# Fifteen products in place of eighteen for six of fc1's tiles, and convolution taps clipped to the image, in a two-layer fp32 kernel

## The chip, the cores and the metric

The kernel runs on one core of a Trainium2 chip, all in fp32. The metric is the device time of one execution in microseconds; the median of eight runs before the change is 3315.88 us (3313.56 to 3318.15). TensorE (PE in the profile) multiplies, VectorE is DVE, ScalarE is ACT, GpSimd is POOL, and SyncE (SP) issues most transfers.

## The reference

Eight images of 384 channels and 32x32 pixels (1024 tokens) go through two layers.

- Layer 0 is a transformer block: layernorm, qkv, attention with 8 heads of 48, projection and residual, layernorm, then an MLP, `fc1` from 384 to 1536 with exact GELU, `fc2` back to 384, and a residual.
- Layer 1 is a ConvNeXt block: a depthwise 7x7 convolution with 3 pixels of zero padding, layernorm over channels, `w1` to 1536, GELU, a global response normalisation (GRN) over the image, `w2` back to 384, and a residual.

The steps that the change touches are these:

```python
h = gelu(einsum('bnc,oc->bno', xn2, w_fc1) + b_fc1)
...
y = conv_general_dilated(x, dw_w, padding=((3, 3), (3, 3)), feature_group_count=DIM) + dw_b
```

## The kernel before

**Layout.** Channels lie on the 128 partitions, tokens along the free axis. 384 channels are three tiles (`CT`), 1536 hidden channels twelve (`HT`), and the 1024 tokens are worked in two halves of 512. The constant `NH` is 512.

**Order of the images.** The loop over images (in `main`, from L1420) is skewed: while image b goes through layer 0, layer 1 of image b-1 follows it. A turn of the loop is: q and k of image b, its attention, its MLP, then `grn_up` (w1) of image b-1, the values of image b+1, and `grn_down` (w2) of image b-1. The depthwise convolution of image b is started behind `grn_up` and runs on DVE beside the values, `grn_down`, and the whole attention of image b+1, up to the MLP of image b+1. The last image (b = 7) has another MLP, `mlp_by_halves`, and its own convolution in two parts of 13 and 19 rows at the end.

**The planner.** Each engine executes its instructions in the order in which the program emits them. `Flow` (L112) decides that order. Every matmul adds its cost to a running clock (`U`, 0.857 us for 512 columns), and chains of other work (generators that yield how long to wait) are resumed when the clock passes their due time. So a yield does not delay an engine; it decides behind which matmul, and between which other DVE instructions, a step stands. `finish` runs the rest of a chain at once. A paced chain counts its waits from when it was due.

**The convolution.** `convolution` (L959) emits 126 taps for a full image, 42 for each channel tile, as one DVE instruction each: acc = window x weight + acc, with a window of the zero-padded copy `pad` (38x38) and 1024 elements. Seven more taps for each channel tile are made by ACT and added by accumulating transfers that POOL issues (`help_convolution`, L985), channel tile after channel tile from the last to the first. While the helper is at a channel tile, and for 8 us after, `convolution` leaves it alone. The helper pauses where `quiet` is set (in w2 and at the averages of the attention). The layernorm of the convolved image (`conv_norm`) waits for the convolution, the helper and the layernorm in front of the MLP.

**fc1 and fc2.** `mlp` (L796) makes the first token half of all 12 hidden tiles, then the second half. A tile and half is three matmuls of 512 columns into one PSUM bank (four such banks rotate) and one GELU from the bank to `hid` (`gelu_half`, L778). Four tiles into the first half come the projection of the second half of the attention and the second half of the layernorm. Two `difference` calls prepare sums for fc2, each a negated copy on ACT and an accumulating transfer from POOL. fc2 and w2 are already made by a scheme of 15 block products in place of 18 (`by_thirds`, `FORMS` at L74): sums of weight blocks, made once, times sums of data blocks, with DVE combining the products.

**Weights.** A ring of nine tiles is loaded in the order of a plan by SP; `used` gives a tile back and issues the next load. An fc1 chunk holds two hidden tiles. During image 0 the chain `prepare` (L1261) makes the weight sums for qk, fc2, w1 and w2 on DVE and stores them to DRAM through POOL; `forms` (L1296) makes the fifteen forms for fc2 and for w2, and w2's come last. `main` finishes `prepare` behind the MLP of image 0 and then starts the first convolution.

Of the kernel before, what the change touches and what calls it, by code (L numbers as in the profile page):

```python
# [46 lines left out]
F32 = mybir.dt.float32  # L47
# [17 lines left out]
CM = 2  # L65
NC = HT // CM
U = 0.857
HELPED = 7
SCALE = HD ** -0.5
EPS0, EPS1, GRN_EPS = 1e-5, 1e-6, 1e-6  # L70
# [81 lines left out]
def block_kernel(  # L152
# [25 lines left out]
    flow = Flow()  # L178
    quiet = []
    s_fc2 = dram.tile([P, len(FORMS), 4 * P], F32, tag="s_fc2", bufs=1, name="s_fc2")  # L180
    s_w2 = dram.tile([P, len(FORMS), 4 * P], F32, tag="s_w2", bufs=1, name="s_w2")
    s_qk = dram.tile([P, CT, 4 * P], F32, tag="s_qk", bufs=1, name="s_qk")
    s_w1 = dram.tile([P, HT // 2, 4, P], F32, tag="s_w1", bufs=1, name="s_w1")

    def half(h):
        return slice(h * NH, (h + 1) * NH)
# [103 lines left out]
    def chunk(w, c):  # L290
        return w[:, c * 6 * P : (c + 1) * 6 * P]
# [1 line left out]

    RAW = ("A11", "A12", "A21", "A22", "A31", "A32")

    def plan_fc1(tag):
        return [((f"fc1_{tag}", c), chunk(wfc1, c)) for c in range(NC)]

    def plan_fc2(tag):
        return [((f"fc2_{tag}", a), chunk(wfc2, c)) for c, a in enumerate(RAW)]  # L300
# [482 lines left out]
    def difference(dst, more, less):  # L783

        nc.scalar.mul(dst, less, -1.0)
        nc.gpsimd.dma_start(out=dst, in_=more, accum_op=ALU.add)
# [5 lines left out]
    def add_first(xt, r, n, bank):  # L792
        dst = xt[:, r, half(n)]
        nc.vector.scalar_tensor_tensor(dst, bank, col("bfc2", r), dst, ALU.add, ALU.add)  # L794

    def mlp(b, xt, xn, weights, tag, ln, rest, before_fc2=None, behind_ln=None):  # L796

        hid = one.tile([P, HT * N], F32, tag="big", name=f"hid_{b}").rearrange("p (m n) -> p m n", m=HT)
        e = [three.tile([P, 2, NH], F32, tag="p", name=f"fc2_e_{b}_{i}") for i in range(2)]
        wa = f"fc1_{tag}"  # L800
        flow.finish(ln)
        for m in range(HT):
            gelu_half(hid, m, 0, xn, weights, wa, f"fc1_{b}")
            if m == 3 and rest:
                rest()
                slow = 1.2 if b == 1 else 1.0
                ln = flow.spawn(layernorm(xt, xn, 1, eps0, "g2", f"ln2_{b}", True, slow=slow))
                behind_ln(ln)
        flow.finish(ln)
        for m in range(HT):  # L810
            gelu_half(hid, m, 1, xn, weights, wa, f"fc1_{b}")
            if m % CM == CM - 1:
                weights.used(wa, m // CM)
            if m in (3, 5):
                two_tiles = hid[:, m - 3 : m - 1, :]
                difference(e[(m - 3) // 2], two_tiles[:, :, half(0)], two_tiles[:, :, half(1)])
        if before_fc2:
            before_fc2()
        bias = lambda r: col("bfc2", r)
        by_thirds(xt, hid, e, True, weights, f"fc2_{tag}", bias, lambda r, n: pad_half(xt, r, n), f"fc2_{b}")  # L820
# [132 lines left out]
    def keep(b, xt):  # L953
# [2 lines left out]
        nc.sync.dma_start(out=kept.rearrange("(c p) n -> p c n", p=P), in_=xt)  # L956
        return kept

    def convolution(acc, us, first=(), y0=0, y1=H, ready=tuple(range(CT)), taken=None):  # L959

        done = [0] * CT
        ct, n = None, 0
        taps = KS * KS - (HELPED if taken is not None else 0)
        while min(done) < taps:
            left = [c for c in ready if done[c] < taps and not (taken and taken.get(c, 0) > flow.now)]
            if not left:
                yield 1.0
                continue  # L970
            ct = min([c for c in left if c != ct] or left, key=lambda c: done[c])
            i = done[ct]
            dy, dx = divmod(i, KS)
            window = pad[:, ct, dy + y0 : dy + y1, dx : dx + W]
            dst = image(acc[:, ct, :])[:, y0:y1, :]
            tap = col("dww", ct * KS * KS + i)
            if i == 0:
                nc.vector.tensor_scalar(dst, window, tap, col("dwb", ct), ALU.mult, ALU.add)  # L978
            else:
                nc.vector.scalar_tensor_tensor(dst, window, tap, dst, ALU.mult, ALU.add)  # L980
            done[ct] += 1
            n += 1
            yield next((early for m, early in first if n <= m), us)

    def help_convolution(acc, us, taken):  # L985

        yield 8.0
        for ct in reversed(range(CT)):
            taken[ct] = float("inf")
            for i in range(KS * KS - HELPED, KS * KS):  # L990
                dy, dx = divmod(i, KS)
                for h in range(2):
                    if quiet:
                        while quiet:
                            yield 1.0
                        yield 3.0
                    t = three.tile([P, NH], F32, tag="res", bufs=4, name=f"tap_{ct}_{i}_{h}")
                    y0 = dy + h * H // 2
                    window = pad[:, ct, y0 : y0 + H // 2, dx : dx + W]
                    tap = col("dww", ct * KS * KS + i)  # L1000
                    nc.scalar.mul(t.rearrange("p (h w) -> p h w", w=W), window, tap)  # L1001
                    nc.gpsimd.dma_start(out=acc[:, ct, half(h)], in_=t, accum_op=ALU.add)  # L1002
                    yield us
            taken[ct] = flow.now + 8.0
        yield 8.0
        taken.clear()
# [254 lines left out]
    def prepare(weights, aside):  # L1261
# [17 lines left out]
        def load_blocks(w, name, *which):  # L1279
            t = one.tile([P, CT, N], F32, tag="acc", name=name).rearrange("p c n -> p (c n)")  # L1280
            parts = []
            for j, (m, k) in enumerate(which):
                parts.append(t[:, j * 4 * P : (j + 1) * 4 * P])
                nc.gpsimd.dma_start(out=parts[j], in_=block_of(w, m, k))
            return parts

        def spare(name):
            return three.tile([P, NH], F32, tag="res", bufs=4, name=name)
# [5 lines left out]
            nc.vector.tensor_tensor(dst, x, y, ALU.add)  # L1294

        def forms(name, w, store):  # L1296
            def keep_form(i, t):
                nc.gpsimd.dma_start(out=store[:, i, :], in_=t)

            a11, a12, a31, a33, a13, a23 = load_blocks(w, f"{name}_a", (1, 1), (1, 2), (3, 1), (3, 3), (1, 3), (2, 3))  # L1300
            x, y, z = (spare(f"{name}_{k}") for k in "xyz")
            yield 16.0
            add(a23, a23, a33)
            add(a11, a11, a12)
            keep_form(6, a11)
            sub(a31, a31, a11)
            keep_form(0, a31)
            yield 2.0
            add(x, a11, a13)
            sub(x, x, a23)  # L1310
            keep_form(8, x)
            nc.vector.scalar_tensor_tensor(y, a11, -1.0, a33, ALU.mult, ALU.subtract)
            keep_form(5, y)
            yield 2.0
            sub(z, a23, a12)
            keep_form(11, z)
            sub(a13, a13, a12)
            sub(a13, a13, a33)
            keep_form(13, a13)
            yield 2.0  # L1320
            nc.vector.tensor_scalar(a12, a12, -1.0, None, ALU.mult)
            keep_form(12, a12)
            nc.vector.tensor_scalar(a23, a23, -1.0, None, ALU.mult)
            keep_form(14, a23)
            a21, a22, a31, a32, a33, a12 = load_blocks(w, f"{name}_b", (2, 1), (2, 2), (3, 1), (3, 2), (3, 3), (1, 2))
            x, y = spare(f"{name}_v"), spare(f"{name}_w")
            nc.gpsimd.dma_start(out=x, in_=block_of(w, 2, 3))
            yield 25.0
            add(x, x, a33)
            sub(y, a22, x)  # L1330
            keep_form(7, y)
            add(a12, a12, a21)
            add(a12, a12, a31)
            keep_form(9, a12)
            yield 2.0
            add(a22, a21, a22)
            sub(a33, a33, a22)
            keep_form(2, a33)
            add(a22, a22, a31)
            keep_form(4, a22)  # L1340
            add(a32, a32, a22)
            keep_form(1, a32)
# [61 lines left out]
            nc.gpsimd.dma_start(out=s_w1[:, :, int(key[1]) - 1, :], in_=t[:, j])  # L1404
        yield from shift_through_w2()
        yield from forms("w2", w2, s_w2)

    def first_values(xn):

# [10 lines left out]
    def main():  # L1420
# [17 lines left out]
        plan = plan_fc1(0) + plan_fc2_fast(0) + plan_qk(1)  # L1438
        for b in range(1, B):
            if b < B - 1:  # L1440
                plan += plan_fc1(b) + plan_fc2_fast(b)
            else:
                for h in range(2):
                    plan += plan_fc1(f"{b}_{h}") + plan_fc2(f"{b}_{h}")
            plan += plan_w1(b - 1, b < B - 1)
            if b == B - 1:
                plan += plan_w1(f"{b}_0", False)
            plan += plan_w2(b - 1, b < B - 1)
            if b < B - 1:
                plan += plan_qk(b + 1)  # L1450
# [74 lines left out]
        for b in range(B):  # L1525
# [22 lines left out]
            flow.finish(state["norm3"])  # L1548
            if b < B - 1:
                y, gx = grn_up(b - 1, acc, weights, b - 1)  # L1550
                start_conv(b, 1.65 if b == B - 2 else 1.7, (26, 2.2), (27, 9.0), (35, 4.4))
                scale = flow.spawn(grn_scale(b - 1, gx, weights, b - 1, y))
                next_values(b + 1)
                flow.finish(scale)
# [166 lines left out]
```

## Time and profile before

| | |
|---|---|
| median of 8 runs | 3315.88 us (3313.56 to 3318.15) |
| the profiled execution | 3316.41 us, its span 3314.6 us |
| TensorE busy | 3278.0 us, 99% |
| DVE busy | 2512.0 us, 76% |
| ACT busy | 1604.2 us, 48% |
| POOL busy | 484.1 us, 15% |
| a turn of the loop, images 3 to 6 | 400.6 us |
| fc1's second half in the fourth image | 1336.4 to 1367.3 us |

Spans of PE's matmuls are modelled at the end: a matmul of 512 columns reads as 0.59 us while the next starts 0.43 us after it. An fp32 matmul stands as two passes, so two records. In a group's line, `out<-in` names the tiles, then come the shapes, the number of instructions, busy time, the mean of one in ns, and the idle time in front of them with what ended most of it. In a timeline a line is: start, duration, engine, line, operation, tiles, how many were merged, and in brackets the idle time in front of the first.

### The profile page before, as it was taken

What the parts mean: (1) busy time and instruction counts of PE and PEld (TensorE: products, weight loads), DVE (VectorE), ACT (ScalarE), POOL (GpSimd) and SP (SyncE); (2) the same over time, 40 slices, a digit from 0 to 9 for tenths busy, and PEclk for the clock granted to TensorE, in tenths of its full rate; (3) what the DMA queues carried; (4) which work ended last, traced back from release to release, by engine and by line L of the source; (5) the groups of instructions that cost most, each with busy time, mean ns of one, the idle gap of its engine ahead of it and who ended that gap; (6) DMA issues with size and microseconds to landing.
All of it is one profiled execution on the core that took longest, in us unless ns stands there. A gap on an engine that the chain in (4) does not pass through costs nothing. (4 is left out here: it accounts for less than half of the span.)

```text
span 3314.6 us, 38765 instructions
## 1 busy us (share of the span) xinstructions
PE 3278.0 (99%) x14296; PEld 1418.0 (43%) x14296; DVE 2512.0 (76%) x3186; ACT 1604.2 (48%) x2194; POOL 484.1 (15%) x569
## 2 busy tenths in 40 slices
PE   8999999999999999999999999999999999999998
PEld 4344444443344433444344443444434443444455
DVE  4445897888967978679786798868886888879950
ACT  2542663447534375353652737526474355623541
POOL 2121210112110121101211022111220112100000
PEclk9999999999999999999999999999999999999999
DMA  5336732647244563537436374273742647333231
GB/s 197 112 107 148 150 67 71 159 114 149 56 104 134 137 127 56 132 106 171 85 58 147 104 182 74 59 176 87 176 77 50 181 104 158 66 74 89 67 97 43
DMA packets 199109, 368.73 MB, mean 111 GB/s; under 512 B 40768, under 2 KB 46784, under 8 KB 198528
## 3 DMA queue, kind: packets, MB, share of 16 engines
q0 software_dynamic: 80896, 158.63, 26.4%
q1 hardware_dynamic: 117728, 206.83, 20.4%
q8 instruction: 115, 1.88, 0.2%
q10 hardware_dynamic: 288, 0.71, 0.1%
q14 instruction: 82, 0.67, 0.1%
HBM read 187.03 MB, written 34.60 MB: 67 GB/s over the span
## 5 line engine op out<-in xcount | busy, mean ns | idle before, releaser
L980 DVE SCALAR_TENSOR_TENSOR acc<-pad,vec,acc 128x1024 f32<-128x1024 f32 x861 | 1069.8, 1277 | 22.2 <-DMA acc<-tap 17.5
L673 ACT ACTIVATE p<-s 128x1024 f32<-128x1024 f32 x512 | 523.7, 1023 | 276.0 <-PE s L664 267.6
L664 PE MATMUL s<-qk 48*64 48x512 f32 x4096 | 544.0, 592 | 1.2 <-ACT p L673 0.9
L684 PE MATMUL o<-p,v 64*64 64x512 f32 x4096 | 541.0, 590 | 0.0
L351 PE MATMUL fc<-xn,fc 128*128 128x512 f32 x1152 | 503.0, 595 | 4.8 <-DVE acc L423 4.8
L1002 POOL DMA_DIRECT2D acc<-tap x294 | 253.9, 887 | 1213.7 <-ACT tap L1001 737.4
L351 PEld LDWEIGHTS fc<-xn,fc 128*128 128x128 f32 x1152 | 218.8, 191 | 284.9 <-issue 276.2
L358 PE MATMUL fc_p<-hid,fc 128*128 128x512 f32 x728 | 318.6, 594 | 0.3 <-DMA hid<-hid 0.3
L370 ACT ACTIVATE hid<-fc,bfc_f 128x512 f32<-128x512 f32 x192 | 131.5, 686 | 346.4 <-PE fc L351 346.3
L684 PEld LDWEIGHTS o<-p,v 64*64 64x64 f32 x4096 | 167.6, 133 | 275.4 <-issue 263.2
L664 PEld LDWEIGHTS s<-qk 48*64 48x64 f32 x4096 | 163.1, 133 | 276.6 <-issue 218.4
L358 PE MATMUL o_p<-y,w 128*128 128x512 f32 x624 | 272.4, 593 | 0.0
L1051 DVE TENSOR_TENSOR y<-h,y 128x512 f32<-128x512 f32 x288 | 197.0, 690 | 90.7 <-PE h L358 76.2
L1001 ACT ACTIVATE tap<-pad,vec 128x512 f32<-128x512 f32 x294 | 210.9, 726 | 26.6 <-DMA acc<-tap 26.5
L358 PEld LDWEIGHTS fc_p<-hid,fc 128*128 128x128 f32 x728 | 137.2, 190 | 179.1 <-issue 166.5
L358 PE MATMUL h<-acc,w_A 128*128 128x512 f32 x432 | 207.3, 595 | 0.0
L980 DVE SCALAR_TENSOR_TENSOR wqkv<-pad,vec,wqkv 128x416 f32<-128x416 f32 (+1 forms) x288 | 193.6, 747 | 0.5
L358 PEld LDWEIGHTS o_p<-y,w 128*128 128x128 f32 x624 | 117.5, 190 | 150.6 <-issue 129.1
L790 ACT COPY pad<-x 128x512 f32<-128x512 f32 x48 | 30.2, 635 | 252.6 <-DVE x L856 187.6
L625 DVE TENSOR_TENSOR attn<-o,attn 128x512 f32<-128x512 f32 x64 | 44.1, 690 | 134.6 <-ACT attn L623 134.6
L549 DVE TENSOR_TENSOR qk<-qk,qk 128x512 f32<-128x512 f32 x168 | 111.5, 687 | 29.1 <-PE qk L358 19.9
L592 PE MATMUL v<-wqkv,xn 128*128 128x384 f32 x384 | 129.0, 494 | 0.0
(311 smaller groups left out, 3750.9 us busy)
## 6 DMA issues: line engine op xcount, KB each, us to landing
acc<-tap POOLq DMA_DIRECT2D x294, 256.0 KB, 3.5
w_A<-in_w SPq DMA_DIRECT2D x72, 384.0 KB
fc<-s_fc SPq DMA_DIRECT2D x91, 256.0 KB
hid<-hid POOLq DMA_DIRECT2D x42, 512.0 KB, 7.2
fc<-in_wfc SPq DMA_DIRECT2D x54, 384.0 KB
w<-s_w SPq DMA_DIRECT2D x78, 256.0 KB
y<-y POOLq DMA_DIRECT2D x36, 512.0 KB, 6.8
kept<-x SPq DMA_DIRECT2D x8, 1536.0 KB
```

The lines of the kernel that those rows point to most:

```text
L351: nc.tensor.matmul(out=ps, lhsT=lhsT(k), rhs=rhs(k)[:, half(h)], start=(k == 0), stop=(k == nk - 1))
L358: nc.tensor.matmul(out=bank, lhsT=lhsT, rhs=rhs, start=k == 0, stop=k == len(pairs) - 1)
L370: nc.scalar.activation(dst, src, function, **kw)
L549: nc.vector.tensor_tensor(dst, bank, part, ALU.add)
L592: nc.tensor.matmul(out=ps[:, :C], lhsT=xn[:, k, t * P : (t + 1) * P], rhs=wv_sb[:, k, :], start=(k == 0), stop=(k == CT - 1),)
L664: nc.tensor.matmul(out=s[64 * i : 64 * i + 64, j, :], lhsT=kT[64 * j : 64 * j + HD, m, k0 : k0 + 64], rhs=qT[64 * j : 64 * j + HD, m, half ...
L673: nc.scalar.activation(p, s, AF.Exp)
L684: nc.tensor.matmul(out=outs[i][64 * j : 64 * j + 64, :], lhsT=v[keys, t, at : at + 64], rhs=p[keys, j, :], start=(t == 0), stop=(t == KT - 1),
L980: nc.vector.scalar_tensor_tensor(dst, window, tap, dst, ALU.mult, ALU.add)
L1001: nc.scalar.mul(t.rearrange("p (h w) -> p h w", w=W), window, tap)
L1002: nc.gpsimd.dma_start(out=acc[:, ct, half(h)], in_=t, accum_op=ALU.add)
L1051: nc.vector.tensor_tensor(dst, bank, part, ALU.add)
```

## The change

- **Taps inside the image.** A tap is computed only where its window lies in the image; the window is taken from the inside of `pad`, and the accumulator is written only there. The centre tap, which covers all, comes first; the helper's seven are those of the middle column and one neighbour of the centre. A tap's wait in the planner is scaled by its size, with a mean of one. The full convolution's base wait goes from 1.7 to 1.58 (1.65 to 1.55 for the one of image 6) and its first 26 from 2.2 to 2.1; that of image 0 stays at 1.6.
- **fc1's last six tiles of the second half**, for images 1 to 6. Each group of three tiles (three rows of weight blocks, three columns of them, and two quarters of 256 tokens) is made by fifteen products of 256 columns with ready weight sums and data sums. Some products add into a bank that ACT or DVE has read already. Thirteen DVE instructions and four ACT copies of 128x256 combine them in `hid`, in place, and the GELU then runs there. The groups stand between plain tiles, and their GELUs are emitted later (`late`). In the first half the tiles 6 to 11 now come first, so their weight chunks are given back in the first half. Ten data sums (`quarter_sums`) of 128x256 are made on DVE behind the layernorm.
- **Weight sums for it**, by `forms`, behind those for w2, with blocks of 256 columns.

The diff, cut:

```diff
+FAST = 2
...
+    def plan_fc1(tag, fast=False):
+        order = [*range(NC // 2, NC), *range(NC // 2)] if fast else range(NC)
+        return [((f"fc1_{tag}", c), chunk(wfc1, c)) for c in order]
...
+    def quarter_sums(xn, t):
+        b11, b12, b21, b22, b31, b32 = (xn[:, k, quarter(n, NH)] for k in range(3) for n in range(2))
+        e, f, h, e2, g, f2, h2, g2, f3, d = t
+        minus = ((e, b11, b12), (f, e, b21), (h, e, b31), (f3, f2, g2), (d, g2, b31))
+        plus = ((e2, h, b12), (g, b22, f), (f2, f, b12), (h2, h, b32), (g2, g, b32))
+        for n, (dst, x, y) in enumerate(minus[:3] + plus + minus[3:]):
+            nc.vector.tensor_tensor(dst, x, y, ALU.subtract if n < 3 or n > 7 else ALU.add)
+            if n % 2:
+                yield 1.0
+    def fc1_group(hid, group, xn, sums, weights, wname, name, late):
...
+        def product(i, ps, more=False):
+            w = weights.at(wname, group, i // 6)[:, i % 6, :]
+            nc.tensor.matmul(out=ps, lhsT=w, rhs=right[i], start=not more, stop=True, skip_group_check=more)
+            flow.pe(U / 2)
+            return ps
...
+        y = product(6, bank("y"))
+        nc.scalar.copy(c11, y)
+        t = product(2, bank("t"))
+        nc.scalar.mul(c21, t, -1.0)
+        x = product(0, bank("x", True))
+        nc.scalar.copy(n16, x)
+        z = product(10, bank("z"))
+        product(5, y, True)
+        lately()
+        product(1, t, True)
+        op(n16, y, n16)
+        x = product(3, bank("u", True))
+        op(c32, x, n16)
+        v_ = product(12, bank("v"))
+        nc.scalar.copy(c12, v_)
+        op(c32, c32, z, ALU.subtract)
+        x = product(4, bank("w", True))
+        lately()
+        op(n17, x, n16)
+        op(c31, t, n17)
+        op(c12, c12, z, ALU.subtract)
+        product(13, y, True)
+        lately()
+        product(11, v_, True)
+        op(c12, y, c12)
+        x = product(14, bank("q", True))
+        op(c11, v_, c11)
+        product(9, v_, True)
+        op(c21, x, c21)
+        product(7, z, True)
+        product(8, x, True)
+        op(n17, v_, n17, ALU.subtract)
+        op(c22, z, n17)
+        op(c21, c21, n17)
+        op(c11, x, c11)
...
+        assert not late
+        late += [gelu(2), gelu(1), gelu(0)]
...
+        for n in range(HT):
+            m = (n + HT // 2) % HT if fast else n
             gelu_half(hid, m, 0, xn, weights, wa, f"fc1_{b}")
...
+                making = flow.spawn(after(ln, quarter_sums(xn, sums), 1)) if fast else None
...
+            plain(0)
+            plain(1)
+            late.append(lambda: difference_of(0))
+            fc1_group(hid, 0, xn, sums, weights, f"fc1f_{tag}", f"fc1_{b}", late)
+            plain(2)
+            fc1_group(hid, 1, xn, sums, weights, f"fc1f_{tag}", f"fc1_{b}", late)
+            plain(3)
+            difference_of(1)
+            for m in (4, 5):
+                plain(m)
+                late.pop(0)()
+            late.pop(0)()
...
+    TAPS = [KS * PAD + PAD] + [i for i in range(KS * KS) if i % KS != PAD and i != KS * PAD + PAD - 1]
+    TAPS += [KS * PAD + PAD - 1] + [i for i in range(KS * KS) if i % KS == PAD and i != KS * PAD + PAD]
+    def inside(dy, dx, y0, y1):
+        rows = slice(max(y0, PAD - dy), min(y1, H + PAD - dy))
+        return rows, slice(max(0, PAD - dx), min(W, W + PAD - dx))
+    def size(dy, dx, y0, y1):
+        rows, cols = inside(dy, dx, y0, y1)
+        return 120 + (rows.stop - rows.start) * (cols.stop - cols.start)
...
-            window = pad[:, ct, dy + y0 : dy + y1, dx : dx + W]
-            dst = image(acc[:, ct, :])[:, y0:y1, :]
-            tap = col("dww", ct * KS * KS + i)
+            rows, cols = inside(dy, dx, y0, y1)
+            window = inner(ct)[:, rows.start + dy - PAD : rows.stop + dy - PAD, cols.start + dx - PAD : cols.stop + dx - PAD]
+            dst = image(acc[:, ct, :])[:, rows, cols]
+            tap = col("dww", ct * KS * KS + TAPS[i])
...
-            yield next((early for m, early in first if n <= m), us)
+            yield share * next((early for m, early in first if n <= m), us)
...
+        yield from forms("fc1", wfc1, s_fc1)
...
-                plan += plan_fc1(b) + plan_fc2_fast(b)
+                plan += plan_fc1(b, True) + plan_fc1_fast(b) + plan_fc2_fast(b)
...
-                start_conv(b, 1.65 if b == B - 2 else 1.7, (26, 2.2), (27, 9.0), (35, 4.4))
+                start_conv(b, 1.55 if b == B - 2 else 1.58, (26, 2.1), (27, 9.0), (35, 4.4))
```

## The prediction

> **What bounds the kernel now.** I read the page's engine shares first, then the timeline of one middle image (the fourth, 1296 to 1421 us), then the last two images, and the granted clock last.
>
> ```profile
> PE 3278.0 (99%) x14296; PEld 1418.0 (43%) x14296; DVE 2512.0 (76%) x3186; ACT 1604.2 (48%) x2194; POOL 484.1 (15%) x569
> L980 DVE SCALAR_TENSOR_TENSOR acc<-pad,vec,acc 128x1024 f32<-128x1024 f32 x861 | 1069.8, 1277 | 22.2 <-DMA acc<-tap 17.5
> L351 PE MATMUL fc<-xn,fc 128*128 128x512 f32 x1152 | 503.0, 595 | 4.8 <-DVE acc L423 4.8
> ```
>
> TensorE sets the time: it is busy for 99%, and the table of waits gives it about 25 us of idle in all, at the start and in the last image. So time falls only where TensorE's own work falls or one of those waits goes; saved DVE time does nothing by itself. The next lines are DVE and PE around fc1's second half (1336.4 to 1367.3 us; start, duration, engine, line).
>
> ```profile
> 1327.78 39.65 PE L351 MATMUL fc<-xn,fc 128*128 128x512 f32 x92
> 1328.79 2.08 DVE L451 SCALAR_TENSOR_TENSOR xn<-xn,vec,ln_rstd 128x512 f32<-128x512 f32 x3 [5.57 <-ACT ln_rstd L448]
> 1330.78 15.81 DVE L980 SCALAR_TENSOR_TENSOR acc<-pad,vec,acc 128x1024 f32<-128x1024 f32 x12
> 1346.62 0.69 DVE L413 TENSOR_TENSOR ln_a<-acc 128x512 f32<-128x512 f32 x1
> 1347.35 0.69 DVE L416 TENSOR_TENSOR ln_a<-ln_a,acc 128x512 f32<-128x512 f32 x1
> ...
> 1368.48 3.68 DVE L423 SCALAR_TENSOR_TENSOR acc<-ln_sum,acc 128x512 f32<-128x512 f32 x6 [19.11 <-PE ln_sum L394]
> ```
>
> One pass takes (39.65 - 0.59) / 91 = 0.429 us, and an fp32 matmul is two passes. DVE owes this half nothing: twelve late taps run ahead of it and then it idles for 19 us. Two exceptions matter (start, duration), and below them five stretches with length, PE busy, granted clock, DMA share and GB/s:
>
> ```profile
> 529.17 27.70 DVE L980 SCALAR_TENSOR_TENSOR acc<-pad,vec,acc 128x1024 f32<-128x1024 f32 x21
> 2937.04 15.81 DVE L980 SCALAR_TENSOR_TENSOR acc<-pad,vec,acc 128x1024 f32<-128x1024 f32 x12 [1.72 <-DMA acc<-tap]
> 2977.49 3.68 DVE L423 SCALAR_TENSOR_TENSOR acc<-ln_sum,acc 128x512 f32<-128x512 f32 x6
> 2979.52 17.72 PE L351 MATMUL fc<-xn,fc 128*128 128x512 f32 x36 [4.82 <-DVE acc L423]
> ```
> ```profile
> 102.81:106.22 3.41, 3.16 (x28) 1.00 0.66 171
> 133.53:136.94 3.41, 3.15 (x32) 0.99 0.17 37
> 136.94:140.36 3.42, 3.42 (x20) 0.51 0.72 231
> 2973.38:2976.79 3.41, 1.32 (x4) 1.00 0.30 99
> 2976.79:2980.21 3.42, 0.69 (x1) 0.50 0.00 0
> ```
>
> In the second image 21 taps are late, not 12. In the last image DVE is behind from 2937 on, so PE waits 4.82 us for a PSUM bank, and half clock follows.
>
> **The change part by part.** The sum is made against the profiled execution, 3316.4 us (span 3314.6 and 1.8 around it), 0.5 above the median.
>
> *Matmuls.* Three tiles cost 9 matmuls, 18 passes, 18 x 0.429 = 7.73 us. Fifteen products of 256 columns cost 30 passes. No 256-column pass with a fresh 128x128 weight is in the trace; at 288 columns 28 passes take 6.95 us, pitch (6.95 - 0.40) / 27 = 0.242, which is 288/512 of 0.429, so the weight load (190 ns busy) is hidden there. I take 0.2155; the upper bound is 0.242, another 9.7 us over 360 passes. A group then takes 6.47, saving 1.26; 12 groups (images 1 to 6, two each) save **15.1 us**.
>
> *Where the groups wait.* Thirteen DVE operations of 128x256 join each group's path. Rows: 128x512 takes 690 ns, 128x128 293 and 128x256 from PSUM 417; so 0.42, spaced 0.34 when independent (six in 2.08 us) and 0.46 when one reads the last (at 512: 0.61 and 0.73). A reader starts 0.2 us after the last column of its product (the residual add starts at 3182.92, PE's modelled end is 3182.89, and the model puts 0.16 behind the last column); PE restarts 0.1 after DVE (a sum that ends at 3184.53 releases PE at 3184.59, one that ends at 2979.37 at 2979.52). Take the group's start as zero, a product as 0.431. The ninth product ends at 3.88, so the fourth operation (n17) starts at 4.08; then c31 4.55, c12-z 4.89, c12 5.35 and c11 5.69 to 6.13. The thirteenth product adds into the bank that c11 read: it is due at 5.18 and starts at 6.2. So even an idle DVE costs **1.1 us a group**. ACT's four copies (128x512 is 579 ns, so about 0.33) end at 4.0 at the latest, before they are needed at 4.3. The gelus now read the finished rows from SBUF, as many as before, each behind at least one plain tile of 2.57 us.
>
> *Taps.* DVE executes in order, so taps put between these operations lengthen the chain. Rows 1277 ns at 1024 elements, 848 at 608 and 647 at 416 give 0.215 + 1.037 per thousand elements; a clipped tap has 909 on average: 1.16 us, 103 us of DVE saved over 861, worth nothing on PE's path itself. Working through the planner: the helper holds channel tile 0 until 8 us behind its last tap, and 12 (second image: 21) taps of it remain, which is what the rows show. With 1.58 for 1.7 the tail is 10, and stays 21 in the second image, whose 1.6 is unchanged. They are due 2.1 us before the second half starts and then every 1.53; group 0 lies 5.1 to 11.6 into the half. Tap seven or eight falls between the third and the fourth operation, the next beside the eighth. One in the chain adds 1.05 and the one ahead of the ninth operation (which the last product awaits) 0.5: **2.6 us** in group 0, with an uncertainty of one tap. Group 1 has none left; the four sums of the layernorm (2.6 us) are done before its first operation can start, so 1.1. In the second image both groups have taps. Stalls: 5 x (2.6 + 1.1) + 2 x 2.6 = **+23.7 us**. Behind them nothing else runs late: the second difference is copied 10 us before its product (5.2 us median to landing), and the ten quarter sums (4.3 us) fit the hole where DVE waits 5.57 for rstd and what follows; without that cover they would delay the first group by as much.
>
> *Clock.* A window with 1.32 of 3.41 us busy was followed by half clock, and one with twelve one-column matmuls too; a like one at 102.81 was not. So some 2 us idle in one window is about the limit. A stall of 2.6 lies in one free-placed window so far in about half the cases. Half clock for 3.41 us costs 1.7: of 7 long stalls 3.5 x 1.7 = **+6.0** (bounds 0 and 12).
>
> The Trainium skill, "TensorE: Matmul & The Clock Gate", Part 1, states that the throttle comes after at least one idle window of about 3.4 us. By that rule no stall here would be gated and the sum would be 6.0 lower, about 3318; the trace's window with 1.32 us busy speaks against reading it so strictly.
>
> *Last image.* DVE's 12 late taps at 1.32 become 10 or 11 at 1.19, then about 26 taps on thirteen rows at 0.55 to 0.6 for 0.66. That is 4 + 2 us earlier at L423, against a wait of 4.82: the wait goes, with the half-clock loss behind it (two windows, some 2.1 us): **-6.9 us**, between -3 and -7. Late next there is gelu L370, which waits behind the pad copy; it has about 1 us to spare. A 0.3 us wait for gmean goes too. The stall at 3182.9 us stays: its chain starts at the residual add behind the last down-projection block, and DVE's backlog (16 us smaller) is not in it.
>
> *Weight sums.* They follow the w2 sums, whose last store is issued at 242 us; 51 us by the planner's waits bring them to 293, ahead of the end of fc2 at 330. Some 20 DVE operations of 0.42, 28 POOL issues of 0.54, and 4 MB of traffic lie in a stretch where DVE idles 38 us; the last ten operations meet fc2's block sums. I put 0, with 0 to +3 as bounds. Each fast image also reads 2 MB more on SP's queue. Three chunks are given back in the first half already, so the six new tiles are asked for 15 us or more before use; a 384 KB load lands in a median of 3.8 us, which is also what a late one would cost.
>
> Sum: -15.1 + 23.7 + 6.0 - 6.9 - 0.3 = **+7.4 us**, or 3323 from the median.
>
> **The rivals.**
> 1. *The chain is free of taps* (faster). If the tail is over before the groups, twelve stalls of 1.1 are left and none is gated: -15.1 + 13.2 - 7.2 = -9, 3307. For it: DVE was idle 19 us here. Against: the tail starts only when the helper ends. It decides from a mean stall under 1.3.
> 2. *Two taps in every chain* (slower). 3.2 us in seven groups and all gated: 7 x 4.9 + 5 x 1.1 - 15.1 - 7.2 = +17.5, 3333. For it: taps at 1.53 us meet a chain of 2.6.
> 3. *The wait in the last image stays*, because another step there is late: 3323 + 7 = 3330.
> 4. *Something at the start or in fc2 is late* (a weight sum issued on POOL ahead of fc2's additions, or the exposed weight loads): +5 to +15, 3328 to 3338.
>
> **How the numbers follow.** Main case 0.45, at 3323, with 3316 to 3330 for one tap or gate more or less; rival 1 0.17; rival 2 0.16; rival 3 0.12; rival 4 0.10. Rival 1 and the upper end of 2 and 4 bound the range: 3308 to 3340. Faster or slower than 0.2% (6.6 us, about what a measurement of this kernel can tell) starts at 3309 and 3322.5. The main case lies on that edge: 0.22 same, 0.21 slower, 0.02 faster. Rival 1 gives 0.13 faster and 0.04 same; rival 2 is slower for 0.13; 3 and 4 for 0.16 and same for 0.06; the remaining 0.03 of rival 2 is same.
>
> **What would show it.** PE waits in front of the thirteenth product on DVE's c11, about 1.1 us in every group, more in group 0; 0.43 us per product in between; windows at half clock behind some of them; no wait on L423 near 2979; the same 7 us near 3183. The prediction is wrong if the groups run without PE waiting, if the late taps are not among their operations, or if the half clock never comes.

## The result

The changed kernel takes 3324.83 us (median of 12 runs, 3321.76 to 3328.13) against 3315.77 us for the one before: ratio 1.0028, 95% interval 1.0020 to 1.0035, so 9 us slower. The profiled execution took 3323.98 us, its span 3322.1 us. Line numbers have moved: L361 is now the plain fc1 matmul (L351 before), L838 and L843 the matmul and the DVE operation of `fc1_group`, L1129 a tap, L368 fc2's matmul, L404 the matmuls of the layernorm's token sums, L996 the accumulating transfers of fc2 and L1459 the store of a weight sum.

The page's engine shares and two groups (busy, mean ns of one, idle in front):

```profile
PE 3272.9 (99%) x14440; PEld 1449.5 (44%) x14440; DVE 2479.4 (75%) x3422; ACT 1618.6 (49%) x2242; POOL 504.6 (15%) x597
L1129 DVE SCALAR_TENSOR_TENSOR acc<-pad,vec,acc 128x899 f32<-128x899 f32 (+8 forms) x861 | 962.9, 1155 | 8.6 <-DMA acc<-tap 5.4
L361 PE MATMUL fc<-xn,fc 128*128 128x512 f32 x936 | 419.1, 603 | 0.0
```

The clipped taps cost 1.155 us each, and DVE spends 107 us less on them in all. The 4.8 us that fc1's matmul waited for L423 is gone from the last line. In PE's table of waits (in total, times, longest) the waits for L843 are new, and those of L404 have grown; the three at L390 and L1299 are the last image's and stood in the kernel before with 11.8, 2.4 and 1.6 us:

```profile
PE fc_v L838 <- DVE hid L843: 18.4, 12, 2.5
PE ln_sum L390 <- DVE ln_a L426: 11.9, 5, 6.0
PE ln_var L404 <- DMA ln_sq<-ln_sq: 3.4, 1, 3.4
PE ln_var L390 <- DVE ln_sq L447: 2.4, 1, 2.4
PE h_last L1299 <- DVE wqkv L461: 1.6, 1, 1.6
PE ln_sum L404 <- DMA ln_a<-ln_a: 1.6, 1, 1.6
PE fc_q L838 <- DVE hid L843: 1.2, 5, 0.2
```

All twelve groups wait once for DVE. DVE beside group 0 of the fourth image (the group starts at 1351.20):

```profile
1354.89 0.42 DVE L843 TENSOR_TENSOR hid<-hid,fc_z 128x256 f32<-128x256 f32 x1
1355.22 1.15 DVE L1129 SCALAR_TENSOR_TENSOR acc<-pad,vec,acc 128x899 f32<-128x899 f32 x1
1356.29 0.42 DVE L843 TENSOR_TENSOR fc_n<-fc_w,fc_n 128x256 f32<-128x256 f32 x1
...
1357.94 0.41 DVE L843 TENSOR_TENSOR hid<-fc_v,hid 128x256 f32<-128x256 f32 x1
1358.27 1.12 DVE L1129 SCALAR_TENSOR_TENSOR acc<-pad,vec,acc 128x870 f32<-128x870 f32 x1
1359.30 0.42 DVE L843 TENSOR_TENSOR hid<-fc_q,hid 128x256 f32<-128x256 f32 x1
```

One tap stands between the third and the fourth operation, and one behind c11 (1357.94). PE beside it, and then the windows of PE's clock (length, PE busy, PEld, DVE, ACT, POOL, granted clock, DMA share, GB/s):

```profile
1355.95 0.59 PE L838 MATMUL fc_q<-hid,fc1f 128*128 128x256 f32 x2
1358.41 0.70 PE L838 MATMUL fc_v<-hid,fc1f 128*128 128x256 f32 x2 [1.86 <-DVE hid L843]
1358.94 0.59 PE L838 MATMUL fc_z<-hid,fc1f 128*128 128x256 f32 x2
1359.77 1.14 PE L838 MATMUL fc_q<-xn,fc1f 128*128 128x256 f32 x2 [0.24 <-DVE hid L843]
```
```profile
1356.49:1359.90 3.41, 1.31 (x6) 0.81 (x6) 3.27 (x8) 0.00 (x0) 0.00 (x0) 1.00 1.08 219
1359.90:1363.31 3.41, 3.41 (x6) 1.67 (x7) 3.19 (x7) 0.00 (x0) 0.00 (x0) 0.50 0.44 147
```

The thirteenth product is due 0.43 us behind the twelfth (1355.95), at 1356.38, and starts at 1358.41: 2.03 us late. The fifteenth is 0.40 late (0.83 behind the fourteenth in place of 0.43). The next window runs at half clock. Group 1 of this image is 1.03 us late, the two groups of the second image 2.41 and 2.68.

By the starts of PE's stages, after against before:

| stage | predicted, us | measured, us |
|---|---|---|
| fc1 of images 1 to 6 (products, stalls, half clock) | +14.6 | +19.7 (image 1 4.75, the others 2.8 to 3.1 each) |
| MLP of image 7 | -6.9 | -6.86 |
| fc2 of image 0 | 0 | +5.25 |
| from the values of images 2 to 7 to their projection (w2, q and k, attention) | 0 | -4.7 (-0.57 to -0.66 each, the last -1.74) |
| start of the kernel | 0 | -1.2 |
| the rest | -0.3 | -1.3 |
| PE's last instruction | +7.4 | +10.9 |

The two profiles end differently: from DVE's last operation to the end of the span 10.4 us went by before and 7.1 after, which makes +7.5 of the 10.9; the medians differ by 9.1.

### The profile page after: what moved, and what is told of

It reads as the page before. It is cut to its first block, busy times and chain, and to the rows that moved or that the text cites. A ratio compares the mean times of both kernels' runs of the same rounds, so it can differ in the third digit from the quotient of the medians.

```text
span 3322.1 us, 39513 instructions
## 1 busy us (share of the span) xinstructions
PE 3272.9 (99%) x14440; PEld 1449.5 (44%) x14440; DVE 2479.4 (75%) x3422; ACT 1618.6 (49%) x2242; POOL 504.6 (15%) x597
## 4 chain that ended last, share of the span: by engine, by line
PE 97%; DVE 2%; DMA 1%; issue 1%; ACT 0%; POOL 0%; DVEq 0%; POOLq 0%; ACTq 0%
PE fc L361 14%; PE s L674 13%; PE o L694 13%; PE h L368 10%; PE fc_p L368 10%; PE o_p L368 9%; PE qk L368 6%; PE v L602 4%; PE proj L616 4%; PE o L1255 4%; PE h_last L1299 2%; PE h L348 2%; PE qk L348 1%; DVE hid L843 1%; PE ln_var L404 1%; PE ln_sum L404 1%
## 5 line engine op out<-in xcount | busy, mean ns | idle before, releaser
L1129 DVE SCALAR_TENSOR_TENSOR acc<-pad,vec,acc 128x899 f32<-128x899 f32 (+8 forms) x861 | 962.9, 1155 | 8.6 <-DMA acc<-tap 5.4
L361 PE MATMUL fc<-xn,fc 128*128 128x512 f32 x936 | 419.1, 603 | 0.0
L368 PE MATMUL fc_p<-hid,fc 128*128 128x512 f32 x728 | 319.2, 595 | 0.0
L361 PEld LDWEIGHTS fc<-xn,fc 128*128 128x128 f32 x936 | 180.2, 194 | 229.3 <-issue 211.3
L380 ACT ACTIVATE hid<-fc,bfc_f 128x512 f32<-128x512 f32 x156 | 106.6, 686 | 353.5 <-PE fc L361 353.4
L368 PE MATMUL o_p<-y,w 128*128 128x512 f32 x624 | 270.9, 592 | 0.0
L368 PEld LDWEIGHTS fc_p<-hid,fc 128*128 128x128 f32 x728 | 138.2, 191 | 177.9 <-issue 173.8
L368 PE MATMUL h<-acc,w_A 128*128 128x512 f32 x432 | 207.3, 595 | 0.0
L368 PEld LDWEIGHTS o_p<-y,w 128*128 128x128 f32 x624 | 118.0, 190 | 148.7 <-issue 132.0
L1129 DVE SCALAR_TENSOR_TENSOR wqkv<-pad,vec,wqkv 128x377 f32<-128x377 f32 (+24 forms) x288 | 177.4, 691 | 0.6
```

What stands on the lines that cost most here:

```text
L361: nc.tensor.matmul(out=ps, lhsT=lhsT(k), rhs=rhs(k)[:, half(h)], start=(k == 0), stop=(k == nk - 1))
L368: nc.tensor.matmul(out=bank, lhsT=lhsT, rhs=rhs, start=k == 0, stop=k == len(pairs) - 1)
```

## The experiments

| kernel | median, us | ratio to before, 95% interval |
|---|---|---|
| the change | 3324.83 | 1.0028 [1.0020, 1.0035] |
| taps only | 3303.95 | 0.9963 [0.9949, 0.9976] |
| fc1 only | 3362.05 | 1.0141 [1.0125, 1.0156] |
| order of the chain | 3301.67 | 0.9953 [0.9940, 0.9967] |
| taps paused | 3309.34 | 0.9980 [0.9971, 0.9989] |
| stall filled | 3315.02 | 0.9996 [0.9987, 1.0005] |
| pace of the last part | 3316.66 | 1.0000 [0.9991, 1.0009] |
| weight sums sooner | 3322.01 | 1.0022 [1.0013, 1.0031] |
| token sums later | 3329.54 | 1.0041 [1.0027, 1.0055] |
| order, pause, sums sooner, pace | 3289.44 | 0.9916 [0.9902, 0.9929] |
| four repairs | 3296.11 | 0.9937 [0.9923, 0.9950] |
| five repairs | 3290.20 | 0.9922 [0.9908, 0.9935] |
| last repairs | 3281.29 | 0.9893 [0.9877, 0.9910] |

The theory was that of the prediction: twelve stalls on DVE's chain, half clock behind the long ones, and clipped taps that pay only in the last image. The rivals were that the taps, not the chain itself, decide the stalls; and, once the result showed it, that image 0's loss is a matter of its own.

### The two parts alone

```diff
-FAST = 2
+FAST = 0
...
-        yield from forms("fc1", wfc1, s_fc1)
...
-                plan += plan_fc1(b, True) + plan_fc1_fast(b) + plan_fc2_fast(b)
+                plan += plan_fc1(b) + plan_fc2_fast(b)
```

> The clipped taps with their new waits, without fc1's groups and their weight sums. Theory (the taps are worth only the wait in the last image): the wait of 4.8 us on L423 and the half clock behind it are gone, nothing else moves on TensorE: 7 to 8 us below the kernel before, about 3308. Rival (shorter taps help in every image): a turn of the loop falls below 400 us as well, 3300 or less. Rival (the wait in the last image went for another reason): 3316.

Measured: 3303.95 us, 4 us below what was expected and faster than both kernels. The last image gives 6.84. Most of the rest lies between the values and the projection of images 2 to 7 (-4.7). In the kernel before, PE waits there twice for DVE each turn: 0.14 us in w2 and 0.22 us in q and k, with 0.10 more for the first pass behind each. With shorter taps neither wait is left, which makes 0.57 us a turn. Eight passes of q and k in the fourth turn, before and in this run:

```profile
1556.35 3.92 PE L358 MATMUL qk<-xn,wqkv 128*128 128x512 f32 x8
```
```profile
1553.13 3.60 PE L367 MATMUL qk<-xn,wqkv 128*128 128x512 f32 x8
```

So the rival that shorter taps help in every image holds in part: from values to values, a turn of images 2 to 5 falls from 400.25 us (the 400.6 given for the kernel before is a little high) to 399.58, but the time stays above 3300. In image 7 a wait of 0.94 us for ACT, 1.17 us in all, goes as well; it is also gone in the next run, which has the old taps, so the taps aren't its cause, and the cause stays open.

```diff
-            rows, cols = inside(dy, dx, y0, y1)
...
+            window = pad[:, ct, dy + y0 : dy + y1, dx : dx + W]
+            dst = image(acc[:, ct, :])[:, y0:y1, :]
...
-1.55 if b == B - 2 else 1.58, (26, 2.1)
+1.65 if b == B - 2 else 1.7, (26, 2.2)
```

> The groups and their weight sums with the old taps and the old waits (twelve late taps of 1.28 us). Theory: the longest stalls get about 0.15 us longer and one more tap can fall into the second group; the wait in the last image is back (about 7 us): 3324.8 + 7 to 10 = 3332 to 3335. Rival (the clipped taps and their waits are what loads the groups): below 3325.

Measured: 3362.05 us, some 28 above what was expected. So the parts don't add: fc1's part costs +46 alone and +21 beside clipped taps (3324.83 - 3303.95). DVE beside group 1 of the fourth image shows why:

```profile
1372.00 3.91 DVE L1128 SCALAR_TENSOR_TENSOR acc<-pad,vec,acc 128x1024 f32<-128x1024 f32 x3
...
1377.94 0.41 DVE L843 TENSOR_TENSOR hid<-hid,fc_z 128x256 f32<-128x256 f32 x1
1378.27 0.68 DVE L423 TENSOR_TENSOR ln_a<-acc 128x512 f32<-128x512 f32 x1
...
1380.93 0.42 DVE L843 TENSOR_TENSOR hid<-fc_y,hid 128x256 f32<-128x256 f32 x1
```

The tail of taps is three taps longer here and ends next to group 1. The layernorm's four sums, 2.66 us, then stand between the sixth and the seventh operation (1377.94 and 1380.93), and group 1 is 3.49 us late instead of 1.03. In the changed kernel these four sums are over (1365.2) before the chain of group 1 begins (1367.01). Half clock follows in these images too, image 1's fc2 loses 5.49 us, and the last image's wait is back. The waits in w2 and in q and k are back too: images 3, 5 and 6 gain 0.01 to 0.02 us there in place of 0.57.

### What the stalls are made of

Order of the chain: the operations up to the one that releases the thirteenth product come first, and those that nothing awaits go behind.

```diff
         op(c32, c32, z, ALU.subtract)
+        op(c12, c12, z, ALU.subtract)
...
         op(n17, x, n16)
-        op(c31, t, n17)
-        op(c12, c12, z, ALU.subtract)
...
-        op(c12, y, c12)
-        x = product(14, bank("q", True))
         op(c11, v_, c11)
-        product(9, v_, True)
+        x = product(14, bank("q", True))
         op(c21, x, c21)
+        op(c12, y, c12)
         product(7, z, True)
+        product(9, v_, True)
+        op(c31, t, n17)
```

> Only the order inside a group is changed: c12-z before n17, c11 and c21 before c12 and c31, and the eighth form's product into z ahead of the one into v. Theory (the stall is the length of DVE's chain up to c11): the second group loses its 1.1 us entirely, the first one with a tap in the chain keeps 0.5 to 1.0 us of its 2.4, no window falls to half clock: 5 x 1.1 + 7 x 1.5 + 7.5 = 23 us below the changed kernel, about 3302. Rival (DVE has too much work there, whatever the order): less than 5 us, 3320 or more.

Measured: 3301.67 us, as expected. PE in the fourth image (both groups' waiting products):

```profile
1352.14 0.70 PE L838 MATMUL fc_v<-hid,fc1f 128*128 128x256 f32 x2 [0.49 <-DVE hid L843]
...
1359.94 0.70 PE L838 MATMUL fc_y<-xn,fc1f 128*128 128x256 f32 x2 [0.21 <-DVE fc_n L843]
```

Group 0 is now 0.65 us late with the same tap in its chain, group 1 0.37 (none was expected), the second image's 1.2 each with one more of 0.8. No half clock follows any of them. Each image gains 3.4 to 4.0 us in fc1.

Taps paused: none is emitted while a group is.

```diff
+            while pause:
+                yield 0.5
             left = [c for c in ready if ...]
```

> No tap is emitted while a group is. Theory: every group stalls 1.1 us, also the first (2.4 before), and no window falls to half clock: 7 x 1.4 + 7.5 = 17 us below the changed kernel, about 3308. Rival (taps only fill time in which DVE waits anyway): no change, 3325.

Measured: 3309.34 us. All twelve groups are late by 1.03 us (1.027 to 1.034), and no half clock follows them: the 1.1 of the prediction is DVE's own chain, and what is above it is taps. The gain was larger than the total shows, because the second image's convolution now ends later (its last tap 6.1 us into fc2, and 4.6 us ahead of it in the changed kernel) and its layernorm's fold transfer is awaited in fc2 (2.1 us, with half clock behind it; 6.1 us in all against the changed kernel).

Stall filled: in the seven groups with a tap in the chain, four products that nothing reads stand in the stall.

```diff
+        for _ in range(4 if not group or name == "fc1_1" else 0):
+            w = weights.at(wname, group, 1)[:, 2, :]
+            nc.tensor.matmul(out=spare_bank[-1][:, 1, : NH // 2], lhsT=w, rhs=b31, start=True, stop=True)
         product(9, v_, True)
```

> Four more products of 256 columns into an unused PSUM bank stand in front of the product that waits for c11, in the seven groups with a long stall; nothing reads them. TensorE is then busy for 1.7 us of the stall, and the chain behind is as long as it was. Theory (an idle TensorE lowers the clock): the six windows at half clock behind the groups go, 6 x 1.3 = 7.6 us below the changed kernel, 3317. Rival (the clock falls for another reason, or the half clock costs nothing because DVE is the limit there): no change or slower by the extra work, 3325 to 3330.

Measured: 3315.02 us. The chain is as late as before, and PE does more work, but the time falls by 9.8 us. PE and the clock in the fourth image (L887 holds the four products, L843 is the matmul of `fc1_group` here):

```profile
1351.50 1.89 PE L887 MATMUL fc_q<-xn,fc1f 128*128 128x256 f32 x8
1353.52 0.70 PE L843 MATMUL fc_v<-hid,fc1f 128*128 128x256 f32 x2
```
```profile
1353.40:1356.80 3.40, 3.04 (x10) 1.82 (x11) 3.30 (x8) 0.00 (x0) 0.00 (x0) 1.00 0.77 173
1356.80:1360.20 3.40, 3.40 (x15) 2.42 (x14) 3.24 (x5) 1.96 (x5) 0.84 (x1) 1.00 0.21 71
```

All six windows at half clock behind the groups are gone. By the starts of fc2, images 1 to 6 gain 9.8 us in this stage: 1.6 us is the price of one.

Pace of the last part of the convolution:

```diff
-                conv = convolution(last, 0.86 if h else 0.66, (), *rows, ready[h])
+                conv = convolution(last, 0.76 if h else 0.66, (), *rows, ready[h])
```

> The second part of the last convolution is emitted every 0.76 us in place of 0.86. Theory (the wait of 7 us at 3193 is the layernorm of the last rows, emitted behind the last residual add, not DVE's backlog): with the layernorm emitted 11 us earlier, and taps short enough for DVE to follow, the 7 us and the half clock of 10 us behind them go: 8 to 12 us below the changed kernel, 3313 to 3317. Rival (DVE's backlog is the limit there): taps emitted sooner change nothing, 3325.

Measured: 3316.66 us. In the changed kernel PE stands still for the last image's layernorm three times near 3195; with the faster pace once, and the 10.2 us at half clock there are gone. That is 5.6 us up to the start of w1's products and 8.0 us over the stage. First the change, then this run:

```profile
3194.49 0.75 PE L390 MATMUL ln_sum<-ln_a,ones 128*128 128x288 f32 x2 [1.70 <-DVE ln_a L426]
3197.69 1.33 PE L390 MATMUL ln_var<-ln_sq,ones 128*128 128x288 f32 x2 [2.45 <-DVE ln_sq L447]
3200.63 7.03 PE L1299 MATMUL h_last<-wqkv,w_A 128*128 128x288 f32 x16 [1.62 <-DVE wqkv L461]
```
```profile
3181.34 0.65 PE L390 MATMUL ln_sum<-ln_a,ones 128*128 128x288 f32 x2
3194.04 2.21 PE L1299 MATMUL h_last<-wqkv,w_A 128*128 128x288 f32 x8 [1.27 <-DVE wqkv L461]
```

So the convolution did bind this wait, but through its planned pace, not through a backlog on DVE: in the changed kernel DVE itself waits 1.00 us for PE in front of the last residual add, behind which the layernorm's sums are emitted (3193.49); in this run they stand ahead of that add (3177.44). The prediction had left the convolution out of that chain; its forecast that the wait stays as it is held.

### The loss in image 0

POOL in the kernel before and, below it, in the changed one:

```profile
292.47 1.22 POOL L865 DMA_DIRECT2D hid<-hid  x1 [2.26 <-PE fc_p L358]
294.19 1.19 POOL L865 DMA_DIRECT2D hid<-hid  x1 [0.51 <-PE fc_p L358]
```
```profile
293.96 1.40 POOL L1459 DMA_DIRECT2D s_fc<-fc_b  x2 [1.25 <-DVE fc_b L1448]
297.41 0.69 POOL L1459 DMA_DIRECT2D s_fc<-fc_b  x1 [2.05 <-PE ln_sum L404]
297.97 2.60 POOL L996 DMA_DIRECT2D hid<-hid  x2
```

Two additions for fc2, issued at 292 to 294 before, now stand behind stores of weight sums and go at 298. The last of these stores (297.41) comes right behind a weight sum on DVE, which has waited for an earlier store to land:

```profile
296.69 0.42 DVE L1451 TENSOR_TENSOR fc_b<-fc_b 128x256 f32<-128x256 f32 x1 [2.56 <-DMA s_fc<-fc_b]
```

PE meanwhile waits for the fold transfers of the next image's layernorm (1.56 us at 295.68, 3.40 at 317.26), with half clock behind the second. The kernel before already waited 0.77 and 0.17 there. The second fold transfer isn't issued late (311.12, and 311.34 before) but takes 6.0 us to land in place of 3.3; the last of the delayed additions lands at 314.6, and at 311.0 before. Two edits take these apart.

```diff
-            yield 16.0
+            yield 10.0 if w is wfc1 else 16.0
...
-            yield 25.0
+            yield 14.0 if w is wfc1 else 25.0
```

> The two long waits of the planner in fc1's weight sums cut (16 to 10 and 25 to 14), so that POOL's last store is issued before fc2 of image 0 starts its additions. Theory (stores on POOL push fc2's additions and the layernorm's folding transfers back): the waits of 1.6 and 3.4 us at 294 and 314 us fall to the 0.8 and 0.2 of before and the half clock at 319 goes: 5 us below the changed kernel, 3319.5. Rival (the extra traffic itself does it, or the new kernel's earlier arrival): no change, 3325.

Measured: 3322.01 us, about 3 us below the change, with intervals that overlap. The additions go at 292.88 and 294.61 again, the second fold transfer lands in 3.2 us, and PE waits 1.23 and 0.28 us for the fold transfers. The half clock near 319, expected to go, stays (at 318.32).

Image 0's fc2 loses 2.35 us here in place of 5.25, but this doesn't show what the edit is worth. Image 0 runs the same code in the change and in five of the other runs (fc1 only, order, pause, filled, pace), and there fc2 loses 5.25, 1.57, 5.85, 2.64, 2.05 and 5.70 us. In three of the six PE waits 3.3 to 3.4 us for the second fold transfer, in the others 0.4 to 1.2. So the weight sums at their old place cost 1.6 to 5.9 us (without them, with the taps only, it is 0.48), and a combination below loses 5.06 with the sums sooner.

```diff
-            norm = abreast(xn, xn, eps0, "g1", name, True, places=places, gentle=b > 0, factor=1.4 if b else 1.7)
+            norm = abreast(xn, xn, eps0, "g1", name, True, places=places, gentle=b > 0, factor=1.4 if b else 1.7, wait=3.4 if b > 1 else 6.0)
```

> The changed kernel, but in the MLPs of images 0 and 1 the layernorm of the next image plans 6.0 us in place of 3.4 between issuing its fold transfers and the matmuls that read them. If the lost 5.25 us of image 0 are these matmuls standing in front of transfers that are not there (1.56 and 3.40 us, and half clock behind), they go, and with them the 0.77 and 0.17 us that the kernel before waits there: 5 to 6 us faster than the changed kernel, 3319 us; no window at half clock near 318, image 0's step between -1 and +0.5. If instead the weight sums hold up fc2's own sums (their additions go through the same POOL queue), image 0 keeps at least 3 of its 5 us: 3322 to 3325. Images 2 to 7 unchanged in both.

Measured: 3329.54 us, slower than the change: both times were missed. The waits for the fold transfers went, as the first theory had it, and image 0's fc2 kept 3.99 us, as the second had it. PE in image 0:

```profile
299.54 0.65 PE L404 MATMUL ln_sum<-ln_a,ones 64*64 64x512 f32 x2
...
312.91 1.96 PE L368 MATMUL fc_p<-hid,fc 128*128 128x512 f32 x4 [0.93 <-DVE attn L444]
316.46 7.99 PE L368 MATMUL fc_p<-hid,fc 128*128 128x512 f32 x18 [1.59 <-DMA hid<-hid]
...
333.90 11.33 PE L602 MATMUL v<-wqkv,xn 128*128 128x384 f32 x29 [3.94 <-DVE xn L461]
```

The token sums wait for nothing now. But fc2 itself waits for its additions, which POOL issues four in a row from 299.87, and the layernorm, 5.2 us later by plan, ends too late for the values, with half clock behind that. So the weight sums hold up image 0 through two queues, POOL's and DVE's, and the layernorm had only about 1.3 us to spare (5.2 - 3.94, an estimate). In image 1 the longer plan was harmful as well (+2.9 us).

### All together

The first combination has the order, the pause, the sums sooner and the pace of 0.76.

> The earlier weight sums, the new order in the groups, the pause of the taps and the faster last part together. Theory: no stall in any group, so a turn of the loop is 400.6 - 2.5 - 0.6 = 397.5 us; 3324.8 - 5 - 36 - 10 = 3274, faster than before by 1.2%. Rival (the gains overlap, or the taps that are put off are late at the layernorm of the convolved image): 3290 or more.

Measured: 3289.44 us, 15 above what was expected. No group waits for DVE any more. By stages against the changed kernel, fc1 and fc2 of images 1 to 6 give 28 us of the 36 expected: order and pause both remove the half clock, so their gains overlap, and image 1's fc2 (+5.49 against the kernel before) waits for a fold transfer. The last image gives 8.0 of 10. Image 0's fc2 gives none of its 5 (+5.06 against the kernel before), with waits of 1.31 and 1.34 us for fold transfers and half clock behind them, though fc2's additions go on time.

The next two take the planned wait of 6.0, one without and one with the pause.

> Four edits together: the chain order, weight sums sooner, the pace of the last convolution part 0.76, and the 6.0 us planned wait of images 0 and 1; taps not paused. By stages of the runs so far: the chain order's 3301.7, minus 5.6 for the last part, minus 3 to 6 for image 0: 3290 to 3293. If the fold waits move elsewhere instead of going, 3296.

> As the one with four edits, and no tap is emitted while a group is. The kernel with all but the 6.0 us wait took 3289.4 us and kept 5.06 us in image 0 and 5.49 us in image 1's fc2, both in front of fold transfers. If the planned wait takes both away: 3280 us, and about 10 us faster than with four edits (1.2 us a turn for five turns, and image 1's). If only image 0's goes, 3284 to 3285; if neither, 3289.

Measured: 3296.11 and 3290.20 us. In both the values of image 1 wait 3.95 us for the layernorm, as above. In the second, image 1's fc2 still waits 1.96 us: that fold belongs to the convolution's layernorm, which this edit doesn't reach.

The last: a planned wait of 4.2 us in image 0 alone, and the pause for images 2 to 6 alone.

```diff
-            pause.append(0)
+            pause.extend([0] * (b > 1))
...
-factor=1.4 if b else 1.7)
+factor=1.4 if b else 1.7, wait=3.4 if b else 4.2)
```

> The kernel with all but the planned wait (3289.4 us), with two changes: taps are paused beside the groups of images 2 to 6 only, and in image 0 the wait planned for the fold transfers is 4.2 us in place of 3.4 (6.0 made the values wait 4 us for the layernorm, so only 1.3 us of the 5.2 that it moved the chain by were spare, and two waits of 0.8 more are the most that fits). Image 1's fc1, fc2 and values should then move by +0.8 us in all against the kernel before as with the chain order alone, instead of +3.4, and image 0's fc2 by 1 to 2.5 instead of 5.06, if no half clock comes there: 3282 to 3284 us. If the additions of fc2 and the fold transfers hold each other up in image 0 whatever the plan, it stays at 5 and the time is 3286 to 3287.

Measured: 3281.29 us, ratio 0.9893 [0.9877, 0.9910], the fastest. Image 0's fc2 is now 2.79 us shorter than in the kernel before, and no window between 141 and 3274 us runs at half clock. PE there:

```profile
297.06 0.65 PE L405 MATMUL ln_sum<-ln_a,ones 64*64 64x512 f32 x2
297.44 0.65 PE L405 MATMUL ln_sum<-attn,ones 64*64 64x512 f32 x2
...
316.67 0.65 PE L405 MATMUL ln_var<-ln_sq,ones 64*64 64x512 f32 x2
316.68 0.65 PE L405 MATMUL ln_var<-attn,ones 64*64 64x512 f32 x2
```

## Why the prediction was right, and where it wasn't

The time (3323 against 3324.8) and its sign were right, in part by luck, as the last steps show. Step by step:

- **Matmuls, -15.1: right.** The products stand 0.431 us apart, which is 0.2155 a pass.
- **Where the groups wait, 1.1 us a group: right.** With no tap beside them the groups are 1.03 us late, and the first pass behind a wait takes 0.1 more.
- **Taps, 2.6 in group 0: right.** 2.03 + 0.10 + 0.40 = 2.53, with the one tap where it was put. Group 1 was due 1.1 and took 1.13. The second image took 2.5 and 2.8 against 2.6. The sum of stalls is 5 x (2.53 + 1.13) + 5.3 = 23.6 against 23.7.
- **Clock, +6.0: the term was mis-sized.** "A stall of 2.6 lies in one free-placed window so far in about half the cases": six of seven were followed by half clock, not 3.5, at 1.6 us each (the filled stalls) and not 1.7: +9.8. In all, -15.1 + 23.6 + 9.8 = +18.3 of the 19.7 measured in fc1; 1.4 us stays open. The Trainium skill, "TensorE: Matmul & The Clock Gate", Part 1, has the throttle come after at least one idle window of about 3.4 us; the runs disagree with a literal reading, since 2.3 to 2.7 us of idle in a window were enough here.
- **Last image, -6.9: right** (-6.86), and the wait on L423 went. The 0.3 us at gmean went too, but the stage it lies in is as long as before (-0.02), so that term was nothing.
- **Weight sums, 0 with 0 to +3 as bounds: this step failed.** Image 0's fc2 lost 5.25 us, and 1.6 to 5.9 in the six traces with the same code there, three of them above the bound. The working placed the sums in time "ahead of the end of fc2" and priced DVE, POOL and traffic apart; it didn't ask what stands behind the stores in POOL's queue (fc2's additions), nor saw that the fold transfers next to them were already late in the kernel before.
- **Taps "worth nothing on PE's path itself": failed.** In w2, q and k they were worth 0.57 us a turn, by waits of 0.14 and 0.22 us that are too short to stand out in the table of waits. From the values to the projection images 2 to 7 became 4.7 us shorter in all, 1.17 of it for a reason that stays open. That the time came out right is thus in part a cancellation: fc1 5.1 and image 0 5.25 above the working, these stages 4.7 and the start and the rest 2.2 below it. The start's 1.2 need not be an effect of the change: over five traces that have the same code there, it spreads by 1.8 us.

Of the rivals, the first's condition (a mean stall under 1.3) didn't hold, at 2.0; but the edited order met it, and 3301.67 shows how close it was. Of the second, the gating came true (six of seven), but not the stalls: 2.5 and 2.8 us in image 1 and 2.53 in the others' group 0, where it had 3.2. The third fell. The fourth's mechanism, a weight sum on POOL ahead of fc2's additions, did happen, at or below the lower end of its price, together with the main case.

## What to carry to other kernels

A product that adds into a bank which another engine still has to read puts that engine's whole queue on TensorE's path: put the operations that release a product first and those that nothing awaits last, and keep background work out of the queue for that time. Here the order alone was worth 23 us and turned a loss into a gain. Work that is hidden by time may still stand in front of something in a queue: for every step that is added, list what is behind it on its engine, and which of those were already late. And with stalls near a clock's limit, count the idle time that falls into one window, not the longest stall: keeping below that limit was worth 9.8 us with no chain shortened.

## What the runs showed of the hardware

- **Half clock follows a window that is idle in part.** Idle time, taken from the starts of PE's passes, over all windows of 3.41 us at full clock between 200 and 3250 us in the fourteen traces, without those that hold 64x64 matmuls: of 36 windows with over 2.16 us idle, all were followed by half clock; of 14 with 2.00 to 2.16, eleven; of 69 with 0.9 to 2.00, none. So the limit lay near 60% of a window. The windows left out don't keep to it: of eight with 64x64 matmuls and 1.37 to 1.88 us idle, four were followed by half clock, and so was one with 1.13. The second image's group 0 in the changed kernel, 2.41 us late, was not followed by one: its stall lay across two windows.
- **The same 64x64 matmuls take half the time when both halves are ready.** In the kernel before, the sums of the first half start at 296.13, those of the second at 297.00, and fc2 goes on at 298.01: 1.88 us. In the last kernel both start at 316.67 and 316.68 and fc2 goes on at 317.68: 1.0 us. This is part of why image 0's fc2 came out 2.8 us shorter than before.
- **The first pass behind a wait takes 0.32 us in place of 0.216**, at every group of the changed kernel.
